# Two passages between stages of an axial-attention kernel rearranged: q sums in four parts and embedding products in a row; scales, score banks and v loads in another place

## The chip, the cores and the metric

The kernel runs on one core of a Trainium2 chip, as one program in one launch. The metric is the time of one execution on the device in microseconds, and what is compared are medians of several runs.

## The reference

The program computes a network of four layers on x with shape (4, 256, 64, 64), in float32. Each layer adds its result to x: x = x + layer(gn(x)), where gn is a group norm over 32 groups. The change touches the first layer alone, an attention along one image axis with 16 groups and a span of 64:

```
N = B * H                                   # 4 * 64 sequences of length W = 64
xp = x.transpose(0, 2, 1, 3).reshape(N, Cin, W)
qkv = bn(einsum('nci,oc->noi', xp, w_qkv))  # batch norm over all N and W
q, k, v = qkv in 16 groups: 8, 8 and 16 channels
q_emb, k_emb, v_emb = rel_emb[:, i - j + 63], split in the same way
qe = einsum('ngci,cij->ngij', q, q_emb)
ke = einsum('ngci,cij->ngij', k, k_emb)
qk = einsum('ngki,ngkj->ngij', qe, ke)
sim = bn(concatenate([qk, qe, ke])).sum of the three
sim = softmax(sim, axis=3)
attn   = einsum('ngij,ngcj->ngci', sim, v)
attn_e = einsum('ngij,cij->ngci', sim, v_emb)
out = bn(attn) + bn(attn_e)
```

All three batch norms take their mean and variance from the data of the whole batch. So the attention falls into stages: the scale of the first norm is known only when all projections are made, that of the second only when all scores are made. Layers 1 to 3 are 3 x 3 convolutions (with ternary weights, with binary inputs, and with weights generated from a small matrix).

## The kernel before

The kernel is written with a tile framework. Instructions are called in the order of the program; a planner with costs of its own decides in which order each engine's queue gets them, so that an instruction called later can come ahead of one called earlier if it is reckoned to be ready sooner. `tc.keep_in_program_order` pins an instruction to its place in the program. Tiles come from pools, and a tile that takes the place of earlier ones waits until their readers and writers are done. DMAs are issued from the queues of SyncE (SP), ScalarE and GpSimd; a DMA that has to wait holds up what stands behind it on its queue.

**Stage one, projections (lines 164 to 382).** A loop over four images b and, in each, eight blocks k of 512 pixels. VectorE normalises a block into `xg` (L285, three buffers). TensorE makes the q and k channels from it (`po`, L293; 256 channels in two tiles, o = 0 and 1) and the v channels (`pv`, L308). ScalarE copies `po` to the image's two tiles `qs` (L296) and `pv` to `vs` (L313), and squares `pv` (L315). VectorE takes the statistics of `po` (L300). At k = 4 the next image is prepared (`normalised`); at k = 1 and 5 of later images VectorE makes a piece of layer 1's ternary weights (`ternary`). At the end of an image `add_up` (L270) sums each q tile over the rows of the image, one reduction of 4096 elements a partition for each of the two tiles (L272), and stores of `qs` to DRAM (`q_d`, L339) go out on SP. For the last image, `add_up` is called only after the statistics of the first batch norm (lines 346 to 372: column sums L348, small matmuls L356 and L360 into `pm`, then `s1` and `c1`), and is pinned. After it all sums are joined into a total (L375), which 16 stores on GpSimd's queue take to `qs_d` (L380).

**From stage one to stage two (lines 407 to 445).** Pools are opened, and the two tables of embeddings are loaded, `rm` and `et` (L423, L425). A loop over eight a makes two products of `et` with itself and with ones. Each of the 16 takes a bank of a pool of two (`psq`), and a VectorE instruction empties each one:

```
for a in range(8):
    ps = psq.tile([P, P], ...)
    nc.tensor.matmul(ps, lhsT=et[:, a, :], rhs=et[:, a, :], ...)
    nc.vector.scalar_tensor_tensor(tb[:, a, :], ps, 8.0, mt[:, M_GRP, :], ...)
    ps = psq.tile([P, 1], ...)
    nc.tensor.matmul(ps, lhsT=et[:, a, :], rhs=mt[0:64, M_ALL, 0:1], ...)
    nc.vector.tensor_scalar(rsum[:, a : a + 1], ps, float(P), ...)
```

`tb` is used by `term_sums` (L479), `rsum` only by the statistics at the end of stage two. Then `spread_scales` (L384) spreads `s1` and `c1` of the first norm over the layout of stage two: small operands on VectorE (L393), matmuls (L395), a copy (L400).

**Stage two, score products (lines 407 to 741).** A loop over 16 q tiles j, each made of eight DMAs from `q_d` (`projections`, L463) into one of four buffers `bqps`. Three of these are single-buffer pools on the right side of SBUF that are opened before stage one; the fourth is opened with stage two. `scaled` (L470, L474) applies the first norm on VectorE. `position_terms` multiplies q blocks by `rm` (L505), 64 matmuls for a pair of banks, and VectorE transposes the banks into the tiles `t` (L512). `product` multiplies these (L526); ScalarE takes them into `o` (L532) and sums squares (L538). Four stores a tile take `o` to `qk_d` on SP (L619); the last tile goes out in two stores at the end (L661). In between go the weights of layers 2 and 3 and, at the third q tile, the reload of the q sums (`load_sums`, L450).

**From stage two to stage three (lines 666 to 741).** After the banks of stage two are closed, VectorE reduces what was gathered, four small matmuls (`pmq`, `pme`) sum it over partitions, and `s2` of the second norm follows. `term_scales` (L716) makes from a coefficient the scale of the position terms: four small VectorE instructions, `spread_scales` with four operands and four matmuls, and a copy. It is called twice, for `se` from the coefficient itself (L731, used only if the attention has to be repeated in a general form) and for `seq` from the coefficient divided by another (L740, used by ScalarE in the first line of stage three).

**Stage three, attention (lines 744 to 1026).** Eight units u (an image and half of the groups). For each of eight k, `next_scores` (L987) calls: `scores` (L849) with, for even k, `terms` (L830: two loads of q blocks `qc` on SP, four scalings on ScalarE, L844), a load of scores `si` of 1 MB on SP (L856), eight matmuls into two tiles `e` of two banks each (L867; pool `pse` holds two such tiles, which is four banks), and two sums `pt` = `e` + `si` on VectorE (L877); then `exponentials` on ScalarE (L907), and `sums` (L911) of the k two before. Three more banks (`pso`, tag "o") hold the products of `values` (`pa`, L945) and `embedded` (`pe`, L970), and one holds the denominators. `load_values` (L817) loads a quarter of a unit's v into `vb` by four DMAs on SP. The order of work is written out:

```
for m in range(4):
    load_values(0, m)
for k in range(NB):
    next_scores(0, k)
for u in range(len(units)):
    ... sums, values of unit u, with load_values(u + 1, k // 2) at odd k
    for k in range(NB):
        embedded(u, k)
        if u + 1 < len(units):
            next_scores(u + 1, k)
```

So the first unit's scores stand alone at the start, with the three banks of `pso` free, and the later units' scores go between the embedded products of the unit before. Then follow the convolutions, which the change doesn't touch.

Of the kernel before, what the change touches and what calls it, by code (L numbers as in the profile page):

```python
# [9 lines left out]
F32 = mybir.dt.float32  # L10
# [3 lines left out]
ALU = mybir.AluOpType  # L14
AX = mybir.AxisListType
# [3 lines left out]
P = 128  # L19
B = 4  # L20
# [21 lines left out]
def network(ctx: ExitStack, tc, x, wqkv, relm, relt, relw, relv, counts, masks, vecs, rowv, ab, w1, l2w1, l2w2, l3w, mats, out):  # L42
# [4 lines left out]
    nc = tc.nc  # L47
# [116 lines left out]
    bqh = ctx.enter_context(ExitStack())  # L164
    bqps = [pool(bqh, f"b_q{i}", side="right") for i in range(3)]
    with ExitStack() as ph:
        wp = pool(ph, "a_w")
        xp_ = pool(ph, "a_x", 6)
        sp = pool(ph, "a_s")
# [10 lines left out]
        mx = sp.tile([P, 2, B], F32, name="mx")  # L180
        qsum = sp.tile([P, 2, B, 64], F32, name="qsum")

# [86 lines left out]

        def add_up(b, qs, pinned=False):  # L270
            for t in range(2):
                total = nc.vector.tensor_reduce(  # L272
                    qsum[:, t, b], qs[t].rearrange("p l a h -> p (l a) h"), AX.X, ALU.add
                )
# [97 lines left out]
        )  # L372
        add_up(B - 1, qs, True)
        qtot = small(sp, [P, 2, 8, 8])
# [35 lines left out]
    with ExitStack() as ph:  # L410
        rp = pool(ph, "b_r")
        bqps += [pool(ph, "b_q3")]
        tp_ = pool(ph, "b_t", 4)
# [13 lines left out]
        tb = rp.tile([P, 8, P], F32, name="tb")  # L427
        rsum = rp.tile([P, 8], F32, name="rsum")
        for a in range(8):
            ps = psq.tile([P, P], F32, name=f"ptb_{a}", tag="pq")  # L430
            nc.tensor.matmul(ps, lhsT=et[:, a, :], rhs=et[:, a, :], start=True, stop=True)
            nc.vector.scalar_tensor_tensor(tb[:, a, :], ps, 8.0, mt[:, M_GRP, :], ALU.mult, ALU.mult)
            ps = psq.tile([P, 1], F32, name=f"prs_{a}", tag="pq")
            nc.tensor.matmul(ps, lhsT=et[:, a, :], rhs=mt[0:64, M_ALL, 0:1], start=True, stop=True)
            nc.vector.tensor_scalar(rsum[:, a : a + 1], ps, float(P), None, ALU.mult)
        xs1 = []
# [302 lines left out]
        nc.vector.tensor_tensor(cq, coef, inv.unsqueeze(1).to_broadcast([P, 2, G]), ALU.mult)  # L739
        seq = term_scales(cq)  # L740
    bqh.close()


    def from_scores(general, keep):
# [67 lines left out]
        def attention(general, good):  # L812
# [36 lines left out]
            def scores(u, k):  # L849

                b, th = units[u]
                if k % 2 == 0:
                    terms(u, k // 2)
                q = qts[u, k // 2]
                si = ip.tile([P, 4, 4, P], F32, name=f"si_{b}_{th}_{k}_{general}", tag="si")
                nc.sync.dma_start(  # L856
                    out=si.rearrange("p a i f -> p a (i f)"),
                    in_=qk_d[b][4 * th : 4 * th + 4].rearrange("a p f -> p a f")[:, :, bass.ts(k, 512)],
                )
                es = [  # L860
                    pse.tile([P, 2, 4, 64, 2], F32, name=f"e_{b}_{th}_{k}_{y}_{general}", tag="e") for y in range(2)
                ]
                for par in range(2):
                    for x_ in range(4):
                        rows = slice(32 * x_, 32 * x_ + 32)
                        i = 8 * k + 2 * x_ + par
                        nc.tensor.matmul(  # L867
                            es[x_ // 2][:, x_ % 2, :, :, par], lhsT=rw[rows, 63 - i : 127 - i].rearrange("p j r -> p (j r)"),
                            rhs=q[rows, :, par, k % 2, :], start=True, stop=True, tile_position=(32 * x_, 0),
                        )  # L870
                for y in range(2):
                    c = 4 * k + 2 * y
                    dst = pt[:, c : c + 2].rearrange("p i a n b -> p i a (n b)")
                    src = si[:, :, 2 * y : 2 * y + 2].rearrange("p a i f -> p i a f")
                    e = es[y].rearrange("p i a n b -> p i a (n b)")
                    if not general:
                        nc.vector.tensor_tensor(dst, e, src, ALU.add)  # L877
# [1019 lines left out]
```

## Time and profile before

| quantity | value |
|---|---|
| time, median of three runs | 2744.98 us (2739.24 to 2749.27) |
| time of the profiled execution | 2735.2 us |
| its span in the profile | 2733.4 us |
| mean granted TensorE clock | 0.943 |
| TensorE matmuls busy | 2393.6 us, 88% |
| TensorE weight loads busy | 1574.3 us, 58% |
| VectorE busy | 1978.0 us, 72% |
| ScalarE busy | 1202.9 us, 44% |
| GpSimd busy | 105.2 us, 4% |
| DMA | 489.86 MB, mean 179 GB/s |
| stage one with its statistics | 0 to about 276 us |
| stage two | 295 to about 890 us |
| stage three | about 903 to 1480 us |
| layers 1 to 3 | about 1480 us to the end |

The profile is a record of one execution on the hardware. Its times are microseconds from the start of the span; "busy" is the time in which an engine had an instruction in work, and weight loads (PEld) overlap matmuls (PE). VectorE is called DVE, ScalarE ACT, GpSimd POOL and SyncE SP. A row of the timeline gives a start, a duration, the engine and line, what the instruction writes and reads, and in square brackets the idle time of the engine before it and what ended that. A row with a count, such as x64, stands for a run of equal instructions that begins at the time given, and its duration is the whole run's. The chain of waits follows the work that ended last back to its releasers. Since the stages hang on each other by the batch norms, the busy shares of the whole span say little on the two passages between them, where the engines take turns; these have to be read in their own stretch.

### The profile page before, as it was taken

Reading aid. Unit: us, or ns where it says so; the run is one execution under the profiler, and the core shown is the slowest. Engines: PE = TensorE matmul, PEld = TensorE weight load, DVE = VectorE, ACT = ScalarE, POOL = GpSimd, SP = SyncE. Lnnn points to the kernel's source line nnn. Section 1 sums busy time; section 2 is a strip of 40 time slices with the busy share of each in tenths; the row PEclk is TensorE's granted clock in tenths of the full one; section 3 lists DMA queues with packets and bytes.
Section 4 is the critical chain, followed back from the end, with each engine's and each line's share of the span. In section 5 each row is a group of like instructions: output and inputs, shape, how many; then the busy total and the mean of one; then the engine's idle time right before and its main releaser. Section 6 shows DMA issues by size and latency. Waiting matters only on the chain.

```text
span 2733.4 us, 78106 instructions
## 1 busy us (share of the span) xinstructions
PE 2393.6 (88%) x34632; PEld 1574.3 (58%) x34632; DVE 1978.0 (72%) x3372; ACT 1202.9 (44%) x1984; POOL 105.2 (4%) x201
## 2 busy tenths in 40 slices
PE   7999788889998788888784999998979859999998
PEld 4666555556666566666663777775545424444443
DVE  6665788888675466666567989887888877867742
ACT  3555245555555644454444656553458411110100
POOL 0000100000001000000000000000000000000000
PEclk9999899999999799989986999999989979999999
DMA  6866366667666877777777556424347742424110
GB/s 237 270 199 194 97 182 183 164 169 189 154 150 150 257 258 251 264 241 256 249 240 265 196 173 201 155 101 155 120 157 255 280 155 92 154 93 139 47 45 33
DMA packets 287996, 489.86 MB, mean 179 GB/s; under 512 B 32737, under 2 KB 149089, under 8 KB 274849
## 3 DMA queue, kind: packets, MB, share of 16 engines
q1 hardware_dynamic: 224992, 359.52, 43.3%
q0 software_dynamic: 14400, 66.53, 6.3%
q10 hardware_dynamic: 48256, 58.73, 6.2%
q8 instruction: 273, 4.47, 0.7%
q14 instruction: 75, 0.61, 0.1%
HBM read 281.46 MB, written 203.23 MB: 177 GB/s over the span
## 4 chain that ended last, share of the span: by engine, by line
issue 36%; PE 34%; DVE 13%; DMA 9%; ACT 5%; SPq 2%; POOL 1%; DVEq 0%; POOLq 0%; ACTq 0%
PE dc L1353 10%; PE pd L505 5%; PE po L293 3%; PE pv L308 3%; DMA at_d<-o_False 3%; PE pq L526 3%; PE e_False L867 2%; DMA x<-x_d 2%; DVE pt L877 2%; PE pa_False L945 1%; PE den_False L918 1%; PE pr_False L936 1%; PE pe_False L970 1%; DMA qc_False<-q_d 1%; DVE e_tr L1446 1%
## 5 line engine op out<-in xcount | busy, mean ns | idle before, releaser
L1066 PE MATMUL gc<-gtr,g_u 128*128 128x512 f32 x1152 | 505.3, 601 | 13.3 <-DVE gtr L1044 6.7
L1066 PEld LDWEIGHTS gc<-gtr,g_u 128*128 128x128 f32 x1152 | 219.9, 192 | 289.9 <-issue 271.2
L512 DVE STREAM_TRANSPOSE t<-pd 128x1024 f32<-128x1024 f32 x256 | 304.4, 1228 | 92.3 <-PE pd L505 87.0
L505 PE MATMUL pd<-rm,qb 64*32 64x256 f32 x8192 | 306.1, 389 | 41.4 <-DVE t L512 33.3
L1457 PE MATMUL pc<-e_tr,e_k 128*64 128x512 bf16 x2304 | 265.2, 391 | 20.3 <-DVE e_tr L1446 13.9
L532 ACT ACTIVATE o<-pq 128x512 f32<-128x512 f32 x256 | 150.4, 593 | 267.2 <-PE pq L526 258.4
L1353 PE MATMUL dc<-dh,d_u 128*128 128x512 f32 x768 | 229.7, 410 | 22.5 <-ACT dh L1330 21.4
L505 PEld LDWEIGHTS pd<-rm,qb 64*32 64x32 f32 x8192 | 169.8, 108 | 133.3 <-DVE t L512 58.8
L907 ACT ACTIVATE pt<-pt,sm 128x512 f32<-128x512 f32 x256 | 162.5, 709 | 174.6 <-DVE pt L877 156.4
L1353 PE MATMUL dc<-dl,d_u 128*128 128x512 f32 x768 | 226.6, 405 | 1.9 <-DVE dl L1331 1.8
L1457 PEld LDWEIGHTS <-e_k 128*64 128x64 bf16 x2304 | 147.4, 112 | 135.1 <-issue 28.7
L526 PEld LDWEIGHTS pq<-t,t 64*64 64x64 f32 x8192 | 144.7, 137 | 88.6 <-issue 71.3
L526 PE MATMUL pq<-t,t 64*64 64x64 f32 x8192 | 166.6, 225 | 31.5 <-issue 26.1
L1353 PEld LDWEIGHTS dc<-dh,d_u 128*128 128x128 f32 x768 | 146.3, 192 | 63.4 <-ACT dh L1330 22.9
L877 DVE TENSOR_TENSOR pt<-e_False,si_False 128x1024 f32<-128x1024 f32 x128 | 151.5, 1215 | 31.9 <-PE e_False L867 26.8
L1084 ACT COPY gc_c<-gc 128x512 f32<-128x512 f32 x32 | 18.6, 580 | 345.5 <-PE gc L1066 345.5
L1353 PEld LDWEIGHTS dc<-dl,d_u 128*128 128x128 f32 x768 | 144.8, 190 | 43.2 <-DVE dl L1331 4.7
L867 PE MATMUL e_False<-qc_False,rw 32*128 32x256 f32 x1024 | 130.7, 476 | 26.5 <-DVE pt L877 13.6
L538 ACT ACTIVATE sq<-o 128x1024 bf16<-128x1024 f32 x128 | 135.3, 1057 | 4.0
L293 PE MATMUL po<-xg,wt 128*128 128x512 f32 x256 | 122.3, 618 | 5.9 <-DVE st L300 4.3
L970 PE MATMUL pe_False<-pt,ve 128*32 128x64 f32 x4096 | 92.6, 246 | 38.2 <-issue 30.7
L308 PE MATMUL pv<-wt,xg 128*128 128x256 f32 x512 | 120.2, 383 | 0.0
(401 smaller groups left out, 3594.6 us busy)
## 6 DMA issues: line engine op xcount, KB each, us to landing
si_False<-qk_d SPq DMA_DIRECT2D x64, 1024.0 KB
qk_d<-o SPq DMA_DIRECT2D x496, 128.0 KB
x<-x_d SPq DMA_DIRECT2D x32, 1056.0 KB
xa<-in_x SPq DMA_DIRECT2D x16, 1024.0 KB
vt_d<-vs ACTq DMA_DIRECT2D x32, 512.0 KB
q_d<-qs SPq DMA_DIRECT2D x64, 256.0 KB
qb<-q_d SPq DMA_DIRECT2D x128, 128.0 KB
qc_False<-q_d SPq DMA_DIRECT2D x64, 256.0 KB
```

The source lines that it names most:

```text
L293: nc.tensor.matmul(psf, lhsT=wt[:, t, bass.ts(o, P)], rhs=xg[:, t, :], start=(t == 0), stop=(t == 1))
L308: nc.tensor.matmul(pv[:, j, :], lhsT=xg[:, t, pix], rhs=wt[:, t, C : 2 * C], start=(t == 0), stop=(t == 1),)
L505: nc.tensor.matmul(pds[t][32 * c : 32 * c + 32, m].rearrange("p j k -> p (j k)"), lhsT=q[rows, 2 * (gp % 2) + g, a, 32 * nb : 32 * nb + 32 ...
L512: nc.vector.transpose(ts[t][:, :, 32 * jh : 32 * jh + 32].rearrange("p a j b -> p j a b"), pds[t].rearrange("p m j k -> p j m k"),)
L526: nc.tensor.matmul(ps[nb][64 * g : 64 * g + 64, m, :], lhsT=ts[1][rows, n // 2, :, n % 2], rhs=ts[0][rows, n // 2, :, n % 2], start=True, ...
L532: nc.scalar.activation(o[:, :, n : n + 8, :], ps[nb].rearrange("p n (a b) -> p a n b", b=2), AF.Copy, accum_out=acc[:, nb, gp, col : col + 1],
L867: nc.tensor.matmul(es[x_ // 2][:, x_ % 2, :, :, par], lhsT=rw[rows, 63 - i : 127 - i].rearrange("p j r -> p (j r)"), rhs=q[rows, :, par, k ...
L877: nc.vector.tensor_tensor(dst, e, src, ALU.add)
L907: nc.scalar.activation(s, s, AF.Exp, scale=s2q[:, gp : gp + 1])
L1066: nc.tensor.matmul(ms[k], lhsT=u[t][:, dx, k, bass.ts(co, P)], rhs=vs[t][:, k, :, dx : dx + 64], start=(first and dx == 0), stop=(last and ...
L1353: nc.tensor.matmul(at[k], lhsT=u[t][:, dx, k, bass.ts(co, P)], rhs=v[:, k, :, dx : dx + 64], start=(first and p_ == 0 and dx == 0), stop=( ...
L1457: nc.tensor.matmul(m[64 * g : 64 * g + 64], lhsT=parts[:, g, i, k, dx, :], rhs=vs[g][:, k, 8 * (q % 2) : 8 * (q % 2) + 8, dx : dx + 64], s ...
```

## The change

In **stage one**, the sums of the last image's q tiles are taken in four parts, called after its blocks 1, 3, 5 and 7, each over 16 of the 64 rows; they are no longer pinned, and the call after the statistics is gone. `qsum` has seven entries instead of four, and the total (L375) reads all seven.

In **the passage to stage two**, the 16 embedding products go in a row into one tile `ptb` of two banks (from the pool `psd` of stage two) and the eight columns of one tile `prs`; two VectorE instructions of four blocks each and one small one then empty them. One of the three early q buffers becomes a buffer of stage two on the left, so that two are early and two are not.

In **the passage to stage three**, `se` is made after `seq`. In the first unit, every third pair of score matrices (tile number 2k + y with remainder 2 by 3) takes two single banks of `pso` in place of one double bank of `pse`, and its sum is made in two halves. The first unit's v loads are called after its scores of k = 1, 3, 5 and 7, one quarter at a time.

```diff
-    bqps = [pool(bqh, f"b_q{i}", side="right") for i in range(3)]
+    bqps = [pool(bqh, f"b_q{i}", side="right") for i in range(2)]
...
-        qsum = sp.tile([P, 2, B, 64], F32, name="qsum")
+        qsum = sp.tile([P, 2, B + 3, 64], F32, name="qsum")
...
-        def add_up(b, qs, pinned=False):
+        def add_up(b, qs, rows=slice(0, 64), part=0):
             for t in range(2):
-                total = nc.vector.tensor_reduce(
-                    qsum[:, t, b], qs[t].rearrange("p l a h -> p (l a) h"), AX.X, ALU.add
-                )
-                if pinned:
-                    tc.keep_in_program_order(total)
+                nc.vector.tensor_reduce(
+                    qsum[:, t, b + part], qs[t].rearrange("p l a h -> p (l a) h")[:, :, rows], AX.X, ALU.add
+                )
...
                 if k == 4 and b + 1 < B:
                     ready = normalised(b + 1)
+                if b == B - 1 and k % 2 == 1:
+                    add_up(b, qs, slice(8 * k - 8, 8 * k + 8), k // 2)
...
-        add_up(B - 1, qs, True)
...
-        bqps += [pool(ph, "b_q3")]
+        bqps += [pool(ph, f"b_q{i}") for i in (2, 3)]
...
+        ptb = psd.tile([P, 8, P], F32, name="ptb", tag="pd")
+        prs = psq.tile([P, 8], F32, name="prs", tag="pq")
         for a in range(8):
-            ps = psq.tile([P, P], F32, name=f"ptb_{a}", tag="pq")
-            nc.tensor.matmul(ps, lhsT=et[:, a, :], rhs=et[:, a, :], start=True, stop=True)
-            nc.vector.scalar_tensor_tensor(tb[:, a, :], ps, 8.0, mt[:, M_GRP, :], ALU.mult, ALU.mult)
-            ps = psq.tile([P, 1], F32, name=f"prs_{a}", tag="pq")
-            nc.tensor.matmul(ps, lhsT=et[:, a, :], rhs=mt[0:64, M_ALL, 0:1], start=True, stop=True)
-            nc.vector.tensor_scalar(rsum[:, a : a + 1], ps, float(P), None, ALU.mult)
+            nc.tensor.matmul(ptb[:, a, :], lhsT=et[:, a, :], rhs=et[:, a, :], start=True, stop=True)
+            nc.tensor.matmul(prs[:, a : a + 1], lhsT=et[:, a, :], rhs=mt[0:64, M_ALL, 0:1], start=True, stop=True)
+        for h in range(2):
+            nc.vector.scalar_tensor_tensor(
+                tb[:, 4 * h : 4 * h + 4], ptb[:, 4 * h : 4 * h + 4], 8.0,
+                mt[:, M_GRP, :].unsqueeze(1).to_broadcast([P, 4, P]), ALU.mult, ALU.mult,
+            )
+        nc.vector.tensor_scalar(rsum, prs, float(P), None, ALU.mult)
...
         coef = s2[:, G : 3 * G].rearrange("p (t g) -> p t g", t=2)
-        se = term_scales(coef)
...
         seq = term_scales(cq)
+        se = term_scales(coef)
...
-                es = [
-                    pse.tile([P, 2, 4, 64, 2], F32, name=f"e_{b}_{th}_{k}_{y}_{general}", tag="e") for y in range(2)
-                ]
+                es = []
+                for y in range(2):
+                    if u == 0 and not general and (2 * k + y) % 3 == 2:
+                        es += [
+                            pso.tile([P, 1, 4, 64, 2], F32, name=f"e_{b}_{th}_{k}_{y}{x_}", tag="o") for x_ in range(2)
+                        ]
+                    else:
+                        e = pse.tile([P, 2, 4, 64, 2], F32, name=f"e_{b}_{th}_{k}_{y}_{general}", tag="e")
+                        es.append(e)
...
-                for y in range(2):
-                    c = 4 * k + 2 * y
-                    dst = pt[:, c : c + 2].rearrange("p i a n b -> p i a (n b)")
-                    src = si[:, :, 2 * y : 2 * y + 2].rearrange("p a i f -> p i a f")
-                    e = es[y].rearrange("p i a n b -> p i a (n b)")
+                at = 0
+                for tile_ in es:
+                    n = tile_.shape[1]
+                    dst = pt[:, 4 * k + at : 4 * k + at + n].rearrange("p i a n b -> p i a (n b)")
+                    src = si[:, :, at : at + n].rearrange("p a i f -> p i a f")
+                    e = tile_.rearrange("p i a n b -> p i a (n b)")
+                    at += n
...
-            for m in range(4):
-                load_values(0, m)
             for k in range(NB):
                 next_scores(0, k)
+                if k % 2 == 1:
+                    load_values(0, k // 2)
```

More of the change, by code (lines that the diff above doesn't have):

```diff
@@ L859, in scores @@
                 )
-                es = [
-                    pse.tile([P, 2, 4, 64, 2], F32, name=f"e_{b}_{th}_{k}_{y}_{general}", tag="e") for y in range(2)
-                ]
+                es = []
[7 more added lines that the diff above has]
+                        es.append(e)
+                rows_of_e = [e[:, i] for e in es for i in range(e.shape[1])]
                 for par in range(2):
@@ L867, in scores @@
                         nc.tensor.matmul(
-                            es[x_ // 2][:, x_ % 2, :, :, par], lhsT=rw[rows, 63 - i : 127 - i].rearrange("p j r -> p (j r)"),
+                            rows_of_e[x_][:, :, :, par], lhsT=rw[rows, 63 - i : 127 - i].rearrange("p j r -> p (j r)"),
                             rhs=q[rows, :, par, k % 2, :], start=True, stop=True, tile_position=(32 * x_, 0),
                         )
-                for y in range(2):
-                    c = 4 * k + 2 * y
-                    dst = pt[:, c : c + 2].rearrange("p i a n b -> p i a (n b)")
-                    src = si[:, :, 2 * y : 2 * y + 2].rearrange("p a i f -> p i a f")
-                    e = es[y].rearrange("p i a n b -> p i a (n b)")
+                at = 0
[5 more added lines that the diff above has]
+                    at += n
                     if not general:
```

## The prediction

> **What bounds the kernel now.** I read the page's chain of waits first, then the chain and the timeline of the two passages, then the table by windows. The stages follow each other, and none hides another, so the change is worth what it takes out of two gaps. The first gap, between stage one (projections) and stage two (score products), in the chain (start us, us, what):
>
> ```profile
> 274.66 0.24 PE pm L360 x2
> ...
> 279.94 8.65 DVE qsum L272 x2
> 288.59 0.07 DVE rsum L435
> ```
>
> VectorE adds up the last image's q tiles (two reductions), and the path passes through them. The timeline of the same stretch (start, us, engine, line; in brackets the idle time before and what ended it):
>
> ```profile
> 276.78 0.54 PEld L434 LDWEIGHTS prs<-mt,et 64*128 64x128 f32 x2
> 277.58 0.49 PEld L431 LDWEIGHTS ptb<-et 64*128 64x128 f32 x2 [0.25 <-DVE tb L432]
> 279.86 8.74 DVE L272 TENSOR_REDUCE qsum<-qs 128x64 f32<-128x4096 f32 x2
> 288.71 0.50 PEld L434 LDWEIGHTS prs<-mt,et 64*128 64x128 f32 x2 [8.29 <-DVE rsum L435]
> 293.07 1.06 PE L395 MATMUL pq<-sm,mt 128*128 128x32 f32 x4 [0.17 <-DVE tb L432]
> 295.00 6.44 PE L505 MATMUL pd<-rm,qb 64*32 64x256 f32 x96 [0.87 <-DVE qb L474]
> 300.85 4.64 DVE L512 STREAM_TRANSPOSE t<-pd 128x1024 f32<-128x1024 f32 x4 [4.48 <-DMA qs_d<-sm]
> ```
>
> To be seen: TensorE makes the embedding products in turns with VectorE (276 to 293) and stands still for 8.3 us behind the reductions; stage two's first matmul starts at 295.00; yet its first transpose starts only at 300.85, because it waits for the stores of the q sums. The second gap, from stage two to three (attention):
>
> ```profile
> 897.82 0.17 DVE L400 COPY sm<-pst 128x16 f32<-128x16 f32 x1 [1.33 <-PE pst L395]
> 901.11 6.00 ACT L844 ACTIVATE qc_False<-qc_False,sm 128x256 f32<-128x256 f32 x12 [7.61 <-DVE sm L400]
> 903.23 2.09 PE L867 MATMUL e_False<-qc_False,rw 32*128 32x256 f32 x16 [2.38 <-ACT qc_False L844]
> 905.36 2.36 DVE L877 TENSOR_TENSOR pt<-e_False,si_False 128x1024 f32<-128x1024 f32 x2 [4.28 <-DMA vb<-vt_d]
> ```
>
> VectorE idles 1.33 us for the scales `se`, which this path doesn't use, before it can make `seq`, on which ScalarE waits. The wait put down to a v load isn't one: the score matmuls that this sum needs end at 903.23 + 2.09 = 905.32, and the sum starts at 905.36. The table by windows (us; busy us of PE, PEld, DVE, ACT, POOL; PE clock, DMA share, GB/s):
>
> ```profile
> 275.00:295.00 20.00, 9.08 (x37) 7.90 (x37) 15.63 (x44) 2.98 (x6) 4.92 (x9) 0.53 0.61 180
> 890.00:903.00 13.00, 4.95 (x20) 4.51 (x20) 5.92 (x37) 3.56 (x8) 0.00 (x0) 0.53 0.98 228
> 903.00:943.00 40.00, 32.37 (x398) 22.99 (x400) 19.71 (x17) 32.61 (x55) 1.98 (x4) 0.80 0.93 297
> ```
>
> Passage one is latency. The first unit of stage three, 903 to 943, is different: ScalarE 32.6 of 40 us, the DMA engines 0.93. Waits between 888 and 945 (us in total, times, longest):
>
> ```profile
> ACT pt L907 <- DVE pt L877: 3.7, 4, 1.5
> ACT qc_False L844 <- DMA qc_False<-q_d: 2.5, 2, 2.1
> ```
>
> [...] by windows the granted clock is 0.50 from 278 on, and full again a little after 300, five us after the matmuls of 295.00. [...] reductions of 128 and 256 elements took 0.29 and 0.42 us, that is 0.16 fixed and 1.03 ns an element. [...] The trace has the order of issue: 16 v loads 890.3 to 907.7, then the score loads.
>
> **The change, part by part.** The sum is made against the profiled execution, 2735.2 us (span 2733.4), which is 9.8 below the median 2744.98; the saving is carried over to the median.
>
> *Sums in four parts.* Removed: 2 x 4.4 us between stages. Added: eight reductions of 1024 elements. By the fit above 0.16 + 1024 x 1.03 ns = 1.2; the L272 reductions, with 64 results, lie within 0.2 of it, so 1.3 each, 2.6 for a pair. Three pairs fall into the last image, where VectorE is idle 31.5 of the 67 us from 205 to 272 while TensorE is busy all along: nothing, as long as the scaled inputs xg (three buffers) stay ahead. Where a pair meets the 4.3 us of ternary weights (k = 1 and 5) it can hold TensorE up by some 2 us each: 0 to 4, I take 0.5. The fourth pair can start at 269.6 and has until the column sums come at 273.35, less 1.0 for L348: 2.7 for 2.6. The last total reads seven pieces instead of four, 1.0 becomes 1.4 to 1.8 (by the fit with its result term, or in proportion); it lies beside the row of products below.
>
> *Products in a row.* 16 products into one two-bank tile and 8 columns of one bank, then 3 VectorE instructions instead of 16. TensorE no longer waits in between; 0.49 + 0.54 = 1.03 us of weight loads for each pair. The row's prs bank is pm's, free at 275.5 as ptb's was (275.57): 275.6 + 8 x 1.03 = 283.8. VectorE's chain to s1, c1 had its square root at 276.1, and without the turns and reductions the spread operands are ready about 278 to 280: under the row. Then as before from 293.07 to 295.00, 1.93 us: stage two starts at 285.7, 9.3 earlier. The products may fill TensorE's holes from 272 (a gain of 2 more), or the planner may put the two halves of tb ahead of the scale chain on VectorE, behind which `scaled` and so all of stage two waits (1.5 less).
>
> *q buffers.* One of three early q tiles moves to the left. By the pools' sizes the first t tile lies 57,120 bytes above the stage's base and the first stage's small tiles begin at about 56,928: that overlap is the 4.48 us wait for qs_d. Afterwards t starts at 65,312, behind those tiles; q buffers 2 and 3 take the place, wanted one and three q tiles after the start (about 25 us and more). What is late next is the matmul itself: at half clock 64 took 3.45 us. The first pair of transposes starts at 285.7 + 3.5 = 289.2; the clock is full at 285.7 + 5.1 = 290.8, so the second 64 end at about 291.8 and their transposes at 294.2. Before: 305.5. Passage one gives 11.3. Bounds: 7 (order wrong, parts not hidden, the reloaded sums of L450 late for VectorE) to 14 (clock stays up).
>
> *Scales.* `se` last: its 4 + 4 + 1 small instructions leave the path, and the 1.33 us hole closes. From 894.2 (s2) five dependent steps to cq at 0.2 each, then 1.3, L395 1.89, copy 0.2: 899.1 against 901.1. Gain 2.0. `se` then has 899 to 901 on TensorE and VectorE, while ScalarE scales the first four q blocks (4 x 0.5): hidden; without that cover up to 1.9.
>
> *Score banks.* Every third score pair uses two free single banks (VectorE halves: 5 x 2 instructions for 5, some 0.05 us more a pair). TensorE can run ahead; the 3.7 us in which ScalarE waited for sums shrinks. Ceiling: ScalarE's own work, and the score loads (five of 1 MB, at 297 GB/s 3.5 us each, from about 907: the last lands near 927, its exponentials end near 936; before 943.5). I take 2.5 of 3.7.
>
> *v loads.* 16 DMAs of 128 KB move on SP from ahead of all scores to behind score blocks 1, 3, 5 and 7. Nothing waits for them until 941.9, so the move gains what SP's order gives, 0.5 of the 2.5 us of waits for q blocks; cost: their 2 MB compete with the score loads, at 297 GB/s up to 7. SP had nothing else ready from 890 to 905, so the planner may issue them there as before: 0.
>
> Passage two: 2.0 + 2.5 + 0.5 = 5, bounds 0 and 10. Sum 11.3 + 5 = 16.3: 2718.9 against this profile, **2728.7** against the median.
>
> **The rivals.** (A) *Only passage one counts*: the v loads fall among the score loads and 2 MB at 297 GB/s = 7 us eats the 5. For it: share 0.93; against: ScalarE is nearer the bound. 2744.98 - 11.3 = 2733.7. (B) *A new wait in place of the old*: parts that hold TensorE up in the last image (4), tb halves ahead of the scales (1.5), the reloaded sums' wait (2): passage one 3.8, with the scales' 2.0: 2739.2, no change. For it: VectorE is in order and the planner's guess of times sets that order. (C) *Slower*: the third stage's seven later units have the same SP queue, where q blocks wait behind score loads (28.1 us in 16 waits, 943 to 1413). If the shifted first unit turns that order round so that each unit's first q block comes 4 us later, that is 28: 2744.98 - 16.3 + 28 = 2756.7. It decides from 24.5 us, 3.5 a unit; below, it is no loss. Against: no later unit's text changes.
>
> **How the numbers follow.** Forecast 0.55, A 0.22, B 0.12, C 0.11. A measurement tells 0.3% (8.2 us) from no change: faster 0.55 + 0.22 = 0.77, same 0.12, slower 0.11. Range: both upper bounds, 24 less, with the 5 by which runs spread, is 2716; upwards to B and the runs' spread, 2742; C and the tail stay out.
>
> **What would show it.** Right: eight reductions of about 1.3 us before 273; no 8 us hole of TensorE; L505 first at about 286 and L512 at about 289, with no wait for qs_d; ScalarE's L844 at about 899; the first unit's values start 5 to 7 us sooner after stage two's end than before. Wrong: L395 late behind tb halves, TensorE waiting on xg in the last image, longer units after the first.

## The result, and the profile after

The changed kernel takes 2731.24 us (median of 17 runs, 2720.99 to 2744.67); before took 2745.41 on the same chips. The ratio is 0.9951, 95% interval 0.9937 to 0.9966: 13.5 us less (9 to 17), where 16.3 were forecast. A second set of runs gave 0.9952 (0.9933 to 0.9970). The profiled execution took 2720.99 us, its span 2719.2 (2733.4 before). The chain of waits of this profile breaks off after its last two pieces, so the passages are read from the timeline.

Lines are numbered anew in the changed kernel: L374, L394, L399, L477, L508 and L515 are the old L375, L395, L400, L474, L505 and L512, and in stage three L847, L877, L889 and L919 the old L844, L867, L877 and L907. Each experiment has numbers of its own; the names of the tiles tell what a line is.

**Passage one**, timeline of the changed kernel (start, us, engine, line; in brackets the idle time before and what ended it). Here and below a view shows only the rows that bear on the reading; rows of other instructions lie between them:

```profile
267.26 1.20 DVE L272 TENSOR_REDUCE qsum<-qs 128x64 f32<-128x1024 f32 x1
269.95 1.20 DVE L272 TENSOR_REDUCE qsum<-qs 128x64 f32<-128x1024 f32 x1
272.00 1.62 DVE L374 TENSOR_REDUCE sm<-qsum 128x128 f32<-128x896 f32 x1
...
276.09 0.21 ACT L106 ACTIVATE sm<-sm 128x4 f32<-128x4 f32 x1 [1.38 <-DVE sm L105]
...
281.69 0.54 PEld L432 LDWEIGHTS prs<-mt,et 64*128 64x128 f32 x2
282.14 1.29 DVE L434 SCALAR_TENSOR_TENSOR tb<-ptb,mt 128x512 f32<-128x512 f32 x2 [6.09 <-PE ptb L431]
283.35 0.17 DVE L108 RECIPROCAL sm<-sm 128x4 f32<-128x4 f32 x1
...
285.05 1.06 PE L394 MATMUL pq<-sm,mt 128*128 128x32 f32 x4 [2.73 <-DVE sm L392]
286.98 8.46 PE L508 MATMUL pd<-rm,qb 64*32 64x256 f32 x150 [0.87 <-DVE qb L477]
291.12 2.38 DVE L515 STREAM_TRANSPOSE t<-pd 128x1024 f32<-128x1024 f32 x2 [2.83 <-PE pd L508]
294.48 2.38 DVE L515 STREAM_TRANSPOSE t<-pd 128x1024 f32<-128x1024 f32 x2 [0.97 <-PE pd L508]
```

To be seen: the sums take 1.20 us each and are done before 272; the hole of 8.3 us and the wait for `qs_d` are gone. But the square root of the scales is there at 276.30, and its reciprocal (L108) comes only at 283.35: VectorE stands for 6.09 us in front of `tb`, for the row of products to end, and the scales are queued behind it. That is a new wait where the old one was.

**Passage two**, the same view:

```profile
884.50 1.89 PE L394 MATMUL pst<-sm,mt 128*128 128x16 f32 x8 [5.00 <-DVE sm L392]
886.63 6.00 ACT L847 ACTIVATE qc_False<-qc_False,sm 128x256 f32<-128x256 f32 x12 [5.72 <-DVE sm L399]
886.65 1.89 PE L394 MATMUL pst<-sm,mt 128*128 128x16 f32 x8 [0.27 <-DVE sm L399]
```

ScalarE's idle time before its first scaling fell from 7.61 to 5.72 us, and the matmuls of `se` now lie beside the scalings. The table by windows over the first unit, and from its values to those of the second, before and then changed:

```profile
901.00:942.00 41.00, 31.36 (x387) 22.03 (x388) 19.78 (x18) 33.50 (x56) 1.98 (x4) 0.79 0.93 295
942.00:1009.00 67.00, 54.85 (x1472) 45.07 (x1471) 41.12 (x50) 32.29 (x54) 3.96 (x8) 0.90 0.78 264
```

```profile
887.00:925.00 38.00, 29.80 (x394) 22.43 (x394) 20.05 (x23) 31.31 (x53) 1.97 (x4) 0.78 0.89 292
925.00:996.00 71.00, 54.86 (x1475) 45.66 (x1474) 41.01 (x50) 34.64 (x58) 3.97 (x8) 0.88 0.82 269
```

The first unit became 3 us shorter, the second 4 us longer.

To see where the time went, the span is cut at marks that each trace has. The columns are two profiles of each kernel and one of each passage alone (`p1_alone` and `p2_alone` below); us:

| stretch | before | before, 2nd | changed | changed, 2nd | passage one alone | passage two alone |
|---|---|---|---|---|---|---|
| to the last `po` matmul's end | 267.8 | 267.9 | 267.3 | 267.8 | 266.6 | 263.4 |
| to the ninth transpose of stage two | 47.9 | 46.9 | 39.7 | 39.7 | 39.7 | 48.1 |
| to the sum over `acc` (end of stage two) | 573.4 | 572.3 | 569.8 | 570.6 | 573.2 | 570.0 |
| to the first scaling of `qc` | 12.1 | 12.2 | 9.8 | 10.1 | 11.7 | 10.2 |
| to the first unit's values | 40.8 | 41.4 | 38.4 | 37.7 | 39.9 | 37.4 |
| to the second unit's values | 67.2 | 67.2 | 70.9 | 70.8 | 66.4 | 70.8 |
| to the last `pe` matmul | 447.3 | 455.6 | 450.0 | 450.2 | 448.2 | 456.1 |
| to the last matmul of layer 3 | 1264.4 | 1265.4 | 1260.6 | 1260.2 | 1260.1 | 1264.7 |

Two profiles of one kernel differ by about 1 us in most rows, and by 8 us in the later units of before, so a smaller difference between single profiles tells little.

### The profile page after: what moved, and what is told of

Same layout as the page of the kernel before. It is cut to its first block, busy times and chain, and to the rows that moved or that the text cites. A ratio compares the mean times of both kernels' runs of the same rounds, so it can differ in the third digit from the quotient of the medians.

```text
span 2719.2 us, 78126 instructions
## 1 busy us (share of the span) xinstructions
PE 2391.5 (88%) x34632; PEld 1578.0 (58%) x34632; DVE 1976.9 (73%) x3370; ACT 1204.6 (44%) x1986; POOL 104.7 (4%) x201
## 5 line engine op out<-in xcount | busy, mean ns | idle before, releaser
L515 DVE STREAM_TRANSPOSE t<-pd 128x1024 f32<-128x1024 f32 x256 | 304.4, 1228 | 86.1 <-PE pd L508 85.2
L508 PE MATMUL pd<-rm,qb 64*32 64x256 f32 x8192 | 307.2, 392 | 41.4 <-DVE t L515 32.3
L1469 PE MATMUL pc<-e_tr,e_k 128*64 128x512 bf16 x2304 | 264.8, 391 | 18.8 <-DVE e_tr L1458 11.7
L508 PEld LDWEIGHTS pd<-rm,qb 64*32 64x32 f32 x8192 | 170.8, 109 | 133.2 <-DVE t L515 58.9
L919 ACT ACTIVATE pt<-pt,sm 128x512 f32<-128x512 f32 x256 | 162.3, 709 | 174.8 <-DVE pt L889 174.8
L529 PE MATMUL pq<-t,t 64*64 64x64 f32 x8192 | 166.9, 224 | 26.7 <-issue 22.2
L889 DVE TENSOR_TENSOR pt<-e_False,si_False 128x1024 f32<-128x1024 f32 x123 | 145.7, 1215 | 26.9 <-PE e_False L877 26.7
L877 PE MATMUL e_False<-qc_False,rw 32*128 32x256 f32 x984 | 128.4, 481 | 28.1 <-DVE pt L889 13.0
L957 PE MATMUL pa_False<-pt,vb 128*32 128x64 f32 x4096 | 100.0, 242 | 25.1 <-DVE o_False L966 18.1
```

The lines of the kernel that those rows point to most:

```text
L508: nc.tensor.matmul(pds[t][32 * c : 32 * c + 32, m].rearrange("p j k -> p (j k)"), lhsT=q[rows, 2 * (gp % 2) + g, a, 32 * nb : 32 * nb + 32 ...
L515: nc.vector.transpose(ts[t][:, :, 32 * jh : 32 * jh + 32].rearrange("p a j b -> p j a b"), pds[t].rearrange("p m j k -> p j m k"),)
L529: nc.tensor.matmul(ps[nb][64 * g : 64 * g + 64, m, :], lhsT=ts[1][rows, n // 2, :, n % 2], rhs=ts[0][rows, n // 2, :, n % 2], start=True, ...
L877: nc.tensor.matmul(rows_of_e[x_][:, :, :, par], lhsT=rw[rows, 63 - i : 127 - i].rearrange("p j r -> p (j r)"), rhs=q[rows, :, par, k % 2, ...
L919: nc.scalar.activation(s, s, AF.Exp, scale=s2q[:, gp : gp + 1])
L1469: nc.tensor.matmul(m[64 * g : 64 * g + 64], lhsT=parts[:, g, i, k, dx, :], rhs=vs[g][:, k, 8 * (q % 2) : 8 * (q % 2) + 8, dx : dx + 64], s ...
```

## The experiments

In what follows, "passage" is the time from the end of the last `po` matmul; where only one number is given, it is to the ninth transpose, when stage two has its full stride.

**The two kernels again.** First `before_again`, with nothing edited:

> The kernel before, once more, for a second profile. In its first profile TensorE stood still at 861.5 for 3.9 us with nothing to wait for and then ran at half clock; from the end of the second pair of first transposes (305.5) to the sum over acc at the end of stage two (889.0) it took 583.5 us, against 579.9 in the changed kernel. If that stop is chance, the second profile has none there and takes 579 to 581; if it belongs to where the code lies, it stands there again and takes 583 to 584.

Measured: TensorE stopped again, a few us later (3.43 us, from 865.8 on), and the same stretch took 582.4 us, between the two ranges named. The clock, which had fallen at the first stop (0.50 from 865 to 870), stayed at 1.00 at this one. So a stop there isn't chance of one execution. But neither passage alone has it there (`p1_alone` and `p2_alone`), and passage one alone takes 583.3 us for this stretch all the same. What makes the stretch longer stays open.

> The changed kernel, once more. In its first profile the first unit's values started 16.8 us sooner than before, those of the sixth only 8.4 sooner, and the end came 14.2 sooner. If the later units give back what the second passage gains, unit lengths of 70.9 (first to second), 66.8, 67.3, 68.0, 71.2 show again and the end is 9 to 12 sooner; if that is chance of one execution, the first to second unit takes 67 to 68 as before. Ratio to before 0.995 either way.

Measured: ratio 0.9952, unit lengths 70.8, 64.8, 66.7, 69.4, 69.4. The longer second unit repeats; the other lengths don't. The give-back is one step, in the second unit.

**Passage one alone** keeps the first three parts of the diff and undoes the last three:

```diff
+        se = term_scales(coef)
         inv = small(sp, [P, G])
...
-        se = term_scales(coef)
...
-                    if u == 0 and not general and (2 * k + y) % 3 == 2:
+                    if False:
...
+            for m in range(4):
+                load_values(0, m)
             for k in range(NB):
                 next_scores(0, k)
-                if k % 2 == 1:
-                    load_values(0, k // 2)
```

> Passage one alone. My theory: stage two's second pair of transposes ends at 296.9 as with the whole change (8.6 sooner than before), stage three keeps its old passage (6.9 us from s2 to the first scaling on ScalarE), and the time is 8.6 less than before, ratio 0.9969. The rival, that passage one is all there is in the end because stage three gives the rest back, has the whole 13.5 here, ratio 0.9951.

Measured: ratio 0.9955 (0.9938 to 0.9972), an interval that holds both expectations. The stretches tell more: the passage is the changed kernel's (39.7), it is 11.7 us from stage two to the first scaling, and layers 1 to 3, which no line of the change touches, take 1260.1 us (1264.4 and 1265.4 before).

**Passage two alone** undoes the sums, the row and the buffer instead (as in the three experiments on them below, together).

> Passage two alone. First transposes at 300.9 with the wait for the q-sum stores, as before; 5.0 us from s2 to the first scaling (6.9 before), and the first values 4 to 4.5 us sooner after s2 than before. If stage three keeps that, the time is 4.2 less, ratio 0.9985; if the later units give it back, 1.000.

Measured: ratio 0.9993 (0.9976 to 1.0009), which holds both expectations. It took 10.2 us to the first scaling, 37.4 to the first values, then 70.8. The first values come 47.6 us after stage two's end (52.9 and 53.6 before). What the first unit gains (some 3 us), the second gives back. Of passage two only the 2 us of the scales remain, which this interval can't tell from nothing.

**The sums undone:**

```diff
-                if b == B - 1 and k % 2 == 1:
-                    add_up(b, qs, slice(8 * k - 8, 8 * k + 8), k // 2)
...
+        add_up(B - 1, qs, True)
         qtot = small(sp, [P, 2, 8, 8])
```

> The whole change, but the last image's q sums in two reductions of 4.4 us at the end, pinned, as before. My theory: in VectorE's queue they stand behind tb and ahead of the spread of the scales, so the whole 8.8 us come on the path behind a row that gains nothing: passage 37 to 38.5, as before. The rival: they fit into the 6.1 us in which VectorE waits for the row, and 2.7 are left on the path: 32 to 33.

Measured: passage 46.5 (39.7 with the parts), second pair's end 36.2, between the two expectations and nearer to mine; ratio 0.9971 (0.9956 to 0.9986). Its timeline:

```profile
278.75 1.29 DVE L435 SCALAR_TENSOR_TENSOR tb<-ptb,mt 128x512 f32<-128x512 f32 x2 [4.56 <-PE ptb L432]
...
280.70 8.74 DVE L272 TENSOR_REDUCE qsum<-qs 128x64 f32<-128x4096 f32 x2
...
290.83 1.06 PE L395 MATMUL pq<-sm,mt 128*128 128x32 f32 x4 [11.90 <-DVE sm L393]
```

The reductions stand behind `tb` and ahead of the spread of the scales, and TensorE waits 11.9 us. The parts are worth 6.8 us.

**The row undone** (the loop of before in place of the row and its three instructions):

```diff
+            ps = psq.tile([P, P], F32, name=f"ptb_{a}", tag="pq")
+            nc.tensor.matmul(ps, lhsT=et[:, a, :], rhs=et[:, a, :], start=True, stop=True)
+            nc.vector.scalar_tensor_tensor(tb[:, a, :], ps, 8.0, mt[:, M_GRP, :], ALU.mult, ALU.mult)
...
-            nc.tensor.matmul(ptb[:, a, :], lhsT=et[:, a, :], rhs=et[:, a, :], start=True, stop=True)
```

> The whole change, but the embedding products in 16 turns with VectorE as before, not in a row. Measured from the end of stage one's last po matmul to the end of the second pair of transposes, the passage takes 37.7, 36.8 and 38.0 us in kernels with the old passage one and 29.6 in those with the new. My theory: the row gives nothing, since VectorE waits for its end (6.1 us) before it makes tb and then the scales; with the sums out of the way the turns take as long: 29 to 30.5. The rival, that the row is a large part of the gain, as the 17.5 us of turns in the profile of before suggest (8.3 of it the hole behind the reductions): 34 or more.

Measured: second pair's end 30.5, ninth transpose 40.6, as my theory has it; the row is worth 0.9 us. Ratio 0.9946 (0.9925 to 0.9967). The turns hold only small waits:

```profile
280.44 0.79 PE L430 MATMUL ptb<-et 64*128 64x128 f32 x2 [0.27 <-DVE tb L431]
281.27 0.29 DVE L431 SCALAR_TENSOR_TENSOR tb<-ptb,mt 128x128 f32<-128x128 f32 x1 [0.82 <-PE ptb L430]
281.62 0.79 PE L430 MATMUL ptb<-et 64*128 64x128 f32 x2 [0.17 <-DVE tb L431]
...
285.00 0.17 DVE L108 RECIPROCAL sm<-sm 128x4 f32<-128x4 f32 x1
```

A turn took 1.18 us against 0.86 in the row, and VectorE could put the scales between the turns.

**The buffer.** Alone, in the kernel before (with stage three in the new wording, its single banks switched off):

```diff
-    bqps = [pool(bqh, f"b_q{i}", side="right") for i in range(3)]
+    bqps = [pool(bqh, f"b_q{i}", side="right") for i in range(2)]
...
-        bqps += [pool(ph, "b_q3")]
+        bqps += [pool(ph, f"b_q{i}") for i in (2, 3)]
```

> The kernel before, with the one q buffer moved and nothing else. The 4.48 us for which the transposes waited for the stores of the q sums go, but stage two's first 64 matmuls take 3.5 us at half clock: first transposes 2.4 us sooner, the second pair's end 1.9 sooner, passage 35.5 to 36. The rival: the whole wait comes back, passage 33. As a second thing, a check on how much the rest moves with a program of other layout: layers 1 to 3 took 1264 to 1265 us in some kernels and 1259 to 1261 in others; if it is the buffer's place that does this, 1260 here.

Measured: second pair's end 37.7, ninth transpose 48.0; ratio 0.9992 (0.9975 to 1.0008); layers 1 to 3 took 1265.1. Both expectations missed, and those for layers 1 to 3 with them (1260 if the buffer's place were the cause):

```profile
297.61 2.38 DVE L512 STREAM_TRANSPOSE t<-pd 128x1024 f32<-128x1024 f32 x2 [2.76 <-PE pd L505]
300.95 2.38 DVE L512 STREAM_TRANSPOSE t<-pd 128x1024 f32<-128x1024 f32 x2 [0.96 <-PE pd L505]
```

The wait for the stores is gone, and in its place the same pairs wait for TensorE, 9.9 us from the first matmul to the second pair's end (10.5 and 9.9 in the two profiles of before). And undone in the changed kernel, with three small additions that make the sums fit into four entries:

```diff
+                if b == B - 1 and k == 0:
+                    for e in (1, 2):
+                        nc.vector.tensor_tensor(qsum[:, :, 0], qsum[:, :, 0], qsum[:, :, e], ALU.add)
...
+                    add_up(0, qs, slice(8 * k - 8, 8 * k + 8), {1: 1, 3: 2, 5: 3, 7: 2}[k])
```

> The whole change, but three early q buffers as before, so that the first t tiles lie on stage one's small tiles again and wait for the stores of the q sums. (So that the sums fit, those of the first three images are added up before the last image, in three more small instructions.) My theory: with the sums in parts the stores have landed by about 287, the transposes start at 291, and the wait is gone anyway: passage 29.5 to 30. The rival, that the buffer is worth the 4.48 us of the wait before: 33 to 34.

Measured: second pair's end 33.9, ninth transpose 44.1; ratio 0.9982 (0.9959 to 1.0005). The number is the rival's, its cause is not:

```profile
296.65 0.29 DVE L683 TENSOR_TENSOR qtot<-qtot,rsum 128x128 f32<-128x128 f32 x1 [6.45 <-DMA qtot<-qs_d]
...
297.38 2.38 DVE L520 STREAM_TRANSPOSE t<-pd 128x1024 f32<-128x1024 f32 x2
```

Here the planner put the product with the *reloaded* sums ahead of the first transposes, and VectorE waits 6.45 us for the reload. Whether the transposes would also have waited for the stores lies under this and stays open.

**The repair of passage one: `tb` last.**

```diff
         scaled(0, qs[0])
+        for h in range(2):
+            tc.keep_in_program_order(
+                nc.vector.scalar_tensor_tensor(
+                    tb[:, 4 * h : 4 * h + 4], ptb[:, 4 * h : 4 * h + 4], 8.0,
...
+        tc.keep_in_program_order(nc.vector.tensor_scalar(rsum, prs, float(P), None, ALU.mult))
```

> The whole change, with the two halves of tb and the small rsum called, and pinned, after the first q tile has been scaled. In the changed kernel VectorE stands idle 6.1 us in front of tb, which waits for the row of products to end at 282.1, and the reciprocal of the scales, whose square root was there at 276.3, comes only after it, at 283.35. My theory, that VectorE's order holds the passage: scales ready long before the row ends, their matmuls at 282.1, stage two's first matmul at about 284.3 (286.98), the second pair of transposes ends at 294.2 (296.9), the whole 2.7 less than with the change. The rival, that TensorE's row holds it: first matmul no earlier than 286.

Measured from stage one's end, which came 3.3 us later in this execution (so that the times named in advance don't fit): first matmul 16.1 (19.7), second pair's end 25.8 (29.6), 3.8 sooner, as my theory has it and more. But the ninth transpose comes at 41.6, 1.9 *later*, and the ratio is 0.9969 (0.9953 to 0.9985). Its timeline and windows show what is late next:

```profile
299.93 0.29 DVE L680 TENSOR_TENSOR qtot<-qtot,rsum 128x128 f32<-128x128 f32 x1 [3.52 <-DMA qtot<-qs_d]
...
302.24 3.64 PE L502 MATMUL pd<-rm,qb 64*32 64x256 f32 x42 [4.09 <-DVE t L509]
```

```profile
295.00:299.00 4.00, 2.82 (x64) 1.64 (x64) 1.41 (x2) 0.00 (x0) 0.00 (x0) 1.00 0.49 180
299.00:302.00 3.00, 0.00 (x0) 0.00 (x0) 1.97 (x5) 0.00 (x0) 0.00 (x0) 0.76 0.01 1
302.00:306.00 4.00, 3.76 (x43) 1.58 (x44) 1.34 (x3) 0.00 (x0) 0.00 (x0) 0.50 0.02 4
```

The reloaded sums come 29.3 us after stage one's end; VectorE now reaches them at 25.8 and waits 3.52. In the changed kernel it reached them at 29.5 and waited for nothing. TensorE stands 4.09 us behind it, the clock falls to 0.50, and 42 matmuls take 3.64 us (1.93 in the changed kernel). By windows of 0.5 us the clock was down from about 300.6, some 2.4 us after TensorE had stopped at 298.15.

**Stage three: the v loads ahead of the scores again, and the banks undone** (each edit as in passage one alone).

> The whole change, but the first unit's v loads ahead of all its scores again. In the changed kernel SP's queue has the three loads d_u of layer 1's weights (1.5 MB) behind the second unit's first four v loads, which wait for the first unit's values; they then go out in the middle of the stores of these values, the sums o wait 6.3 us for a store, and the second unit's values come 70.9 and 70.8 us after the first's (67.2 before). Here d_u is ahead of the v loads again. If that order is the cause: first to second unit 66.5 to 67.5, and from the first scaling to the second unit's values 105 to 106 instead of 108.5 to 109.3, a gain of 3 over the changed kernel. If the second unit is bound by the DMA engines' work as a whole: still 108 to 109.

Measured: the three loads `d_u` go out at 923.7 and 929.1, ahead of the v loads, and the second unit follows in 66.4 us, about as expected (66.5 to 67.5). But the first values come 42.3 us after the first scaling (37.7 and 38.4), so it is 108.7 to the second unit's values: the expected gain isn't there. Ratio 0.9942 (0.9922 to 0.9962). SP's queue and VectorE in the first unit:

```profile
880.46 17.62 SPq L824 DMA_DIRECT2D vb<-vt_d  x16
898.18 3.03 SPq L859 DMA_DIRECT2D si_False<-qk_d  x3
```

```profile
905.48 2.36 DVE L889 TENSOR_TENSOR pt<-e_False,si_False 128x1024 f32<-128x1024 f32 x2 [4.66 <-DMA si_False<-qk_d]
```

The score loads stand behind the v loads, and the sums, which the single banks let run ahead, wait 4.66 us for them; in the changed kernel, where six of the sixteen v loads still go out ahead of the scores and the score loads begin at 893.26, the longest such wait is 1.54.

> The whole change without the single banks for the first unit's scores. If the banks are worth what I forecast (2.5 us), the first scaling to the first values takes 40.3 to 41 us (37.7 and 38.4 with them); if the shorter time comes from the order of loads, it stays below 38.5. In the total nothing outside 1 us, because the second unit takes it up.

Measured: 39.6 to the first values, between the two ranges I gave; second unit 67.6, ratio 0.9936 (0.9912 to 0.9959). With v first and no banks it was 39.9 to 41.4 in four profiles (before twice, passage one alone, the buffer alone; mean 40.6). So the moved v loads alone give about 1, which is no more than profiles of one kernel differ by, the banks give nothing without the moved loads (42.3), and the two together give about 3.

**Both repairs in one kernel** (`tb` last, v loads first):

> tb after the first scaling, and the first unit's v loads ahead of the scores: the two repairs in one. If both act: second pair of transposes ends at 294.2, first to second unit 67, and the time 5.5 to 6 less than with the change alone, ratio to before 0.993.

Measured: 0.9948 (0.9928 to 0.9968). Second pair's end 26.7, but ninth transpose 40.9, with a wait of 2.8 us for the reloaded sums; 41.0 to the first values and 68.7 to the second unit's. No kernel here is shown to be faster than the change as it was made: all these intervals overlap.

## Why the prediction came out right, and where its steps failed

The time, 2731.2, lies near the 2728.7 forecast, but the agreement is in good part luck: passage one gave less than I took, passage two kept some 1 to 2 of its 5 us, and 4.7 of the 14.2 us came from stretches that I had not counted.

*The sums in parts: right.* 1.20 us each (1.3 forecast), beside TensorE, which waited for none of its inputs: the last `po` matmul ended at 267.3 and 267.8 (267.8 and 267.9 before). The total took 1.62 (1.4 to 1.8). They are worth 6.8 of the passage's 7.9 us (47.6, the mean of the three profiles with the old passage in the table, to 39.7).

*The row of products: the failed step of passage one.* The row ran from 275.0 to 282.3, a little better than I reckoned (275.6 to 283.8). What failed is the sentence that the spread operands are ready at about 278 to 280, under the row. I had named the case (two halves of `tb` ahead of the scales, 1.5 less) and set it aside. It happened, and cost more than 1.5: with `tb` last the second pair ended 3.8 sooner. The row by itself gives 0.9.

*From the first matmul to the second pair's end* I reckoned 8.5 us and had 9.9, and both halves were taken too short. The first transposes began 4.1 us after the first matmul (3.5 reckoned): in the old trace the 64th matmul *starts* 3.43 us after the first, but it ends 4.06 after, and the transposes need its end. The second pair began 3.4 later (2.6 reckoned), in part because the clock rose after some 5.5 us and not after 5.1 (0.50 up to 292, 0.88 from there to 294). In the profiled pair the later first matmul (286.98 for 285.7) and these 1.4 us are the difference between the 11.3 forecast and the 8.6 measured (305.5 to 296.9). Counted from the end of stage one to the ninth transpose the passage gave 7.9. Both lie inside my bounds of 7 to 14.

The 5.1 was one draw: over the 14 profiles the clock was up between 2.8 and 6.0 us after the first of these matmuls, so the time of one profile was thin ground for this step.

*The buffer: the mechanism right, its worth nothing alone.* The wait for `qs_d` went, and the matmuls took its place, as the text said for the case with the rest; in the kernel before, 48.0 against 47.6.

*The scales: right.* 2.0 forecast; 12.1 and 12.2 became 9.8 and 10.1. (The steps named in its sum add up to 898.6, not to the 899.1 given; it is the 2.0 that was met.) With the first unit's 3.1 (next point) its values start 5.3 sooner after stage two's end, where 5 to 7 were to show it right.

*Banks and v loads: right in the sum at the place by luck, wrong in the shares, and wrong for the end.* Forecast 2.5 + 0.5; the first values came 3.1 sooner after the first scaling (41.1 to 38.05, means of two). A sum in two halves took 1.28 us and a whole one 1.22, close to the forecast. But the 2.5 were to come out of ScalarE's waits for the sums (3.7 us before), and in the changed kernel these waits stand as they were:

```profile
ACT pt L919 <- DVE pt L889: 3.9, 3, 2.1
```

With the loads moved and no banks they are 7.2 us, so by that one profile the banks take away a wait that the moved loads bring, not the one that was there. About half of the 3.1 us is something else: ahead of the first values ScalarE makes 23 scalings of `qc` in each of the six profiles with the v loads first, and 20 in each of the eight with the loads moved. It is busy for 33.4 us there before and for 31.8 changed; the other three scalings fall into the second unit. So some 1.6 us is work that went past the mark and wasn't saved.

The share of the loads was mis-sized too: "nothing waits for them until 941.9" looked at who needs the v loads, not at what stands behind them in the queue. With v first SP issued the 16 v loads from 880.46 on and the first score loads at 898.18, and a sum waited 4.66 us for one of these. And the step that a gain in the first unit reaches the end failed. Before, SP issued the three loads `d_u` of layer 1's weights (512 KB each) like this:

```profile
932.51 0.69 SPq L1247 DMA_DIRECT2D d_u<-u_d  x1
939.51 0.98 SPq L1247 DMA_DIRECT2D d_u<-u_d  x2
947.51 20.80 SPq L821 DMA_DIRECT2D vb<-vt_d  x16
```

Changed, four v loads of the second unit, which wait for the first unit's values, stand ahead of it, and SP issued nothing for 4.8 us before them (924.96 to 929.78):

```profile
929.78 2.58 SPq L824 DMA_DIRECT2D vb<-vt_d  x4
933.06 2.88 SPq L1259 DMA_DIRECT2D d_u<-u_d  x3
937.25 16.71 SPq L824 DMA_DIRECT2D vb<-vt_d  x12
```

These 1.5 MB now go out among the stores of the values, and the sums `o` wait up to 6.3 us for a store (1.4 and 3.3 in the two profiles of before):

```profile
944.07 0.69 DVE L966 TENSOR_TENSOR o_False<-pa_False,rb 128x512 f32<-128x512 f32 x1 [6.28 <-DMA at_d<-o_False]
```

In all seven profiles with the three `d_u` behind these v loads the longest such wait is 5.1 to 6.3 us and the second unit takes 70.0 to 71.5; in the other seven, where at least one `d_u` is ahead, it is 1.4 to 3.3 and 66.4 to 69.7. This is a small form of my rival C: the shift did turn SP's order round, at one unit and for 3.6 us, not at seven. But with the old order (v first) the time to the second unit's values stayed the same, 108.7. Over all 14 profiles it was 106.3 to 109.9, and by the windows about the same bytes pass in it: 41 us x 295 + 67 x 264 = 29.8 MB before, 38 x 292 + 71 x 269 = 30.2 changed, 42.5 x 291 + 66 x 269 = 30.1 with v first. What isn't moved in the first unit is moved in the second. That the DMA engines set this time is an inference from these sums, and not the only one: ScalarE's work over the two units is equal too (65.80 us before, 65.95 changed). No run took bytes or work away. So rival A gave the right account of the end (passage two counts for little), for a reason near to its own.

*What no step foresaw:* layers 1 to 3 took 1260.2 and 1260.6 us, 4.5 less than before, though nothing in them is edited. It repeats within a kernel and comes and goes between kernels: 1259 to 1261 in four of the kernels that hold the new passage one, 1262 to 1265 in three others that hold it too (row, sums, or banks undone), 1264.0 with `tb` last, 1268.5 with the buffer undone. It goes with the program as a whole; by what in it, stays open. In the profiled pair: 0.5 (stage one) + 8.2 (passage) + 3.6 (rest of stage two) + 2.3 (scales) + 2.4 - 3.7 (first and second unit) - 2.7 (later units) + 3.8 (layers 1 to 3) = 14.4, for 14.2 measured; the rest is rounding. Of these, 8.2, 2.3 and the pair of units are the change at work, as the experiments show. The rest of stage two is not: it took 570.0 us with passage two alone, whose edits all come after it, and 573.2 with passage one alone. Together with the later units and layers 1 to 3 it makes 4.7 us, a third of the whole gain. No run gives the cause of these, and they helped the forecast by chance.

## What to carry to other kernels

Work that is made free for one engine is only as early as its place in the next engine's queue (here `tb`, in front of which VectorE stood for 6.09 us, with the scales behind it): ask where the instruction that empties the row will stand, and what stands behind it. When a wait is removed, name the next arrival on the same engine and its time (here the reloaded sums, 29.3 us after stage one), since it caps the gain; and look at the clock there: TensorE's stop of 4.09 us at that point went with a fall to 0.50. Where two stretches share the transfers, follow a gain past the next place at which all loads have to be there before it is counted (here 3 us gained in the first unit, 4 lost in the second).

## What the runs showed of the hardware that was not expected

The dense row of 16 small products didn't bring the clock up. From 276 to 282 TensorE was busy 6.0 of 6.0 us by the record (which models the ends of matmuls), and the granted clock stayed at 0.50, while the 64-by-32 matmuls from 286.98 on had it up after some 5.5 us (columns: busy us of PE, PEld, DVE, ACT, POOL; clock, DMA share, GB/s):

```profile
280.00:282.00 2.00, 2.00 (x12) 2.00 (x11) 0.00 (x0) 0.00 (x0) 1.32 (x3) 0.50 0.98 254
292.00:294.00 2.00, 2.00 (x58) 1.27 (x55) 1.51 (x2) 0.00 (x0) 0.00 (x0) 0.88 0.56 208
```

Nor do rise and fall keep to one time. The same matmuls had the clock up after 2.8 us in the second profile of before and after 6.0 with the row undone. A stop of 3.33 us in the kernel with both repairs was followed by the fall, 0.8 us after TensorE had started again; a stop of 3.43 us in the second profile of before was not (1.00 in every window from 860 to 885).
